# A windowed-attention kernel with its matmul groups in another order, the norm's short steps on GpSimd, and its last slots drawn by hand

## The chip, the cores and the metric

The kernel runs on one core of one Trainium2 chip. The metric is the device time of one execution in microseconds (us); lower is better. All data are 32-bit floats but for small masks.

## What is computed

First comes a layer of plain causal attention (16 heads of 64, model width 128) on x of shape 4 x 512 x 128, with a layernorm ahead of it. Then come six layers of local attention, each with a feed-forward part (FFN):

```python
for i in range(DEPTH):                      # 6
    x = attn_layer(shift_tokens(x), ...) + x
    x = ffn_layer(shift_tokens(x), ...) + x
# attn_layer: q, k, v = x @ Wqkv; q, k l2-normed per head, scaled, rotated;
#   windows of 32 queries see 64 keys; softmax; times v; @ Wo
# ffn_layer: layernorm; hg = xn @ W1 + b1; a * gelu(gate) @ W2 + b2   (341 wide)
```

`shift_tokens` moves half of the 128 channels by one token. The result of these layers is added to their input.

## The kernel before, in words

A **unit** is 128 tokens of one sequence in one layer of local attention: 6 layers x 4 sequences x 4 tiles (T = 0 to 3) = 96 units. Each unit takes three **slots**. In slot n, `slot` (L840) works on up to four units at once: `new` (n+2) is projected to q, k and v and rotated; `nxt` (n+1) has its q and k transposed; `u` (n) gets scores, exponents, product with V; `prev` (n-1) goes through wo and gets its residual. Everything runs under a manual schedule: each engine executes its instructions in the order of the program text, so the order of the calls in `slot` is the order of the work.

TensorE (PE) runs, per slot: `scores` (L643: 8 mask matmuls and 64 small ones, recorded as 128), `do_project` for q, `project_out_2` (L714, wo), `do_project` for v, `transpose_p` (L680), `do_project` for k, the first half of the product with V (`times_v`, L685: 32 small matmuls a half, recorded as 64), `transpose_q` (L627), the second half, `transpose_k` (L632), and `transpose_o` (L709). Between these stand parts of an FFN. An FFN belongs to a whole sequence (512 tokens, four units) and is spread over seven slots: shift in T=0, `mean` in T=1, `var` in T=2, `scale` in T=3, GEGLU chunks 0, 1, 2 at the ends of the slots T=3, 0, 1, and `out` at the end of the slot T=2. So each slot holds one GEGLU chunk or the output of some FFN, and all but T=0 one step of norm.

PSUM: three tiles of two banks (`two0` to `two2`), turned by one each slot by `part`, hold scores, q, k, v, both halves of the product with V, and the GEGLU chunks (`two_t`, L492; `project` uses (1, 2, 0) for q, k, v). One-bank tiles (`one_t`, L496, two in turn) hold wo's output, norm's results and four-block transposes: wo's output takes one, and the second half of `transpose_p` (L622, `transposed`) takes the same bank two allocations later.

VectorE (DVE) runs the maximum and the subtraction of the scores (L670, L672), sums of squares (L530), residuals (L725), rotations (L535, L539), the division after V (L701, L702), the starts of the inverse norms (L554, L80, L81), and the FFN's gates. ScalarE (ACT) runs squares (L525), exponents (L678), copies out of PSUM (L604, L625) and gelu. GpSimd (POOL) runs `add_rotated` (L550), the twelve steps L83 to L86 of `rsqrt` for the norms of q and k (`inverse_norms`, L552), `over_norm` (L558) and `carry_k` (L641). In the FFN's norm the same twelve steps are on DVE. SyncE (SP) issues the DMAs: 14 to 16 for each unit's V windows (L612 to L616), and the weights of the next layer after the last use of each.

The loop goes on for 7 slots after the last unit's, in which only the rest of the last FFNs is left; `finish` (L773) adds the layers' input, transposes and stores.

Of the kernel before, what the change touches and what calls it, by code (L numbers as in the profile page):

```python
# [32 lines left out]
def body(ctx: ExitStack, tc: tile.TileContext, a, out: bass.AP):  # L33
# [41 lines left out]
    def rsqrt(v, n, eng):  # L75

        y = small.tile([P, n], F32, tag=f"y{n}", name="y")
        t = small.tile([P, n], F32, tag=f"yt{n}", name="yt")
# [9 lines left out]
    def layernorm_steps(state, bank, inT, outT, g=None, b=None, eng=nc.vector):  # L88

        def mean():
            m = bank()
            mm(m, lhsT=avg, rhs=inT(), start=True, stop=True)  # L94
            xc = state["xc"] = tmpt()
            nc.vector.tensor_tensor(xc, inT(), m, ALU.subtract)
            sq = state["sq"] = tmpt()
            nc.scalar.activation(sq, xc, AF.Square)

        def var():  # L100
            v = bank()
            for t in range(NT):
                mm(v[:, t : t + 1], lhsT=state["sq"][:, t * P : (t + 1) * P], rhs=avg[:, 0:1], start=True, stop=True)  # L103
            rs = state["rs"] = small.tile([P, NT], F32, tag="rs", name="rs")
            nc.vector.tensor_scalar(rs, v[:, 0:NT], EPS, None, ALU.add)
            rsqrt(rs, NT, eng)

        def scale():
            bc = bank()
            for t in range(NT):  # L110
# [34 lines left out]
    def shift_into(dst, src):  # L145
# [3 lines left out]
        nc.gpsimd.tensor_copy(dst[HD:P, 1:S], src[HD:P, 0 : S - 1])  # L149
# [361 lines left out]
    def project(u, j):  # L511
        p = two_t((1, 2, 0)[j], "ps_proj")
# [172 lines left out]
    def times_v(u, g):  # L685
        if g == 0:
            u.on = s2.tile([P, NC, 2, HD], F32, tag="on", name="on", bufs=1)
        o = two_t(g, "ps_att")
# [41 lines left out]
    class Ffn:  # L730
        def __init__(self, i, b):
            self.i, self.b, self.us, self.st = i, b, [], {}
# [4 lines left out]
                lambda: s2.tile([P, S], F32, tag="hT", name="hT", bufs=2),  # L737
                vecs[:, i, 0:1],
                vecs[:, i, 1:2],
            )  # L740

        def shift(self):
            self.xs = tmpt()
            shift_into(self.xs, xT[self.b])

        def chunk(self, f):
            i, (f0, fn), h = self.i, FCH[f], self.st["h"]
            w1 = ffn_w[0][0]
            gp = two_t(0, "ps_proj")
            mm(gp[0:fn, 0, :], lhsT=w1[:, DH + f0 : DH + f0 + fn], rhs=h, start=True, stop=True)  # L750
            mm(gp[0:fn, 1, :], lhsT=w1[:, f0 : f0 + fn], rhs=h, start=True, stop=True)  # L751
            g = tmpt()
            nc.scalar.activation(g[0:fn, :], gp[0:fn, 0, :], AF.Gelu, bias=vecs[0:fn, i, 6 + f : 7 + f])
            u = tmpt()
            nc.vector.scalar_tensor_tensor(
                u[0:fn, :], gp[0:fn, 1, :], vecs[0:fn, i, 3 + f : 4 + f], g[0:fn, :], ALU.add, ALU.mult
            )
            self.us.append(u)

        def out(self):  # L760
            w2 = ffn_w[0][1]
            y = two_t(0, "ps_proj")[:, 0, :]
            for f, (f0, fn) in enumerate(FCH):
                mm(y, lhsT=w2[0:fn, f, :], rhs=self.us[f][0:fn, :], start=(f == 0), stop=(f == len(FCH) - 1))  # L764
            xn = new_xT()
            nc.vector.scalar_tensor_tensor(xn, y, vecs[:, self.i, 2:3], xT[self.b], ALU.add, ALU.add)
            xT[self.b] = xn
            if self.i + 1 == L:
                self.finish(xn)
            elif self.b + 1 == B:  # L770
                ffn_w[0] = load_ffn(self.i + 1)

        def finish(self, xn):  # L773
            fin = tmpt()
            nc.vector.tensor_tensor(fin, x1T[self.b], xn, ALU.add)
            op = one_t()
            for t in range(NT):
                nc.tensor.transpose(op[:, t * P : (t + 1) * P], fin[:, t * P : (t + 1) * P], ident)
            ot = tmpt()
            nc.scalar.copy(ot, op)  # L780
            nc.sync.dma_start(
                out=out[self.b].rearrange("(t p) e -> p t e", p=P),
# [57 lines left out]
    def slot(n, now, last):  # L840
# [4 lines left out]
        T = n % NT  # L845
        part[0] = n % 3
        begin(unit(n + 4))
        if u:
            scores(u)
        if new:  # L850
# [5 lines left out]
        if u:  # L856
            exponents(u)
# [4 lines left out]
        if new:  # L862
            sum_squares(new, 0)
        if prev:
            residual(prev)
        if now and T > 0:
            (now.mean, now.var, now.scale)[T - 1]()
        if now and T == 0:
            now.shift()
        if new:  # L870
            rotate(new, 0)
        if n == -1:
            residual1(B - 1, y)
        if new:
            do_project(new, 2)
            v_windows(new, follower(new))
        if u:
            transpose_p(u)
        if new:
            add_rotated(new, 0)  # L880
            do_project(new, 1)
            square(new, 1)
        if u:
            times_v(u, 0)
        if new:
            sum_squares(new, 1)
        if nxt:
            transpose_q(nxt)
        if u:
            times_v(u, 1)  # L890
        if new:
            inverse_norms(new)
            over_norm(new, 0)
        if nxt:
            transpose_k(nxt)
        if new:
            rotate(new, 1)
            add_rotated(new, 1)
            over_norm(new, 1)
# [4 lines left out]
        if now and T == 3:  # L904
            now.chunk(0)
        if last:
            (lambda: last.chunk(1), lambda: last.chunk(2), last.out)[T]()
# [3 lines left out]
    with tc.manual_schedule():  # L911
        begin(units[0])
        ffns = {}
        late = norm_x1(one_t, B - 1)
        first_slot()
        for n in range(-1, len(units) + NT + 3):
            if 1 <= n < 4:
                late[n - 1]()
            q = n // NT - 1
            if n % NT == 0 and 0 <= q < L * B:  # L920
# [95 lines left out]
```

## Time and profile before

| what | value |
|---|---|
| median of 3 runs | 2271.33 us (2264.25 to 2271.35) |
| profiled execution | 2271.15 us, its span 2269.1 us |
| granted TensorE clock | 0.992 |
| PE, DVE, POOL, ACT busy | 96%, 75%, 64%, 60% of the span |
| slot of unit 4 starts, slot of unit 88 starts | 639.45, 2099.09 us |
| slot of unit 94 starts | 2206.40 us |

The plain attention takes the first 570 us or so and is the same in both kernels. After it slots follow each other every 16 to 19 us. In the rows of a timeline, the first number is the start in us from the span's start, the second the length; "[0.80 <-DVE t L539]" is idle time of that engine just before the row, and what ended it. "issue" stands for idle time in which the engine waited for nothing that the profile shows. Ends of matmuls are modelled.

### The profile page before, as it was taken

How to read it: one execution, taken by the hardware profiler on the slowest of the kernel's cores; microseconds unless marked ns; L12 is line 12 of the kernel's file. 1: busy time of each engine (PE TensorE's matmuls, PEld its weight loads, DVE VectorE, ACT ScalarE, POOL GpSimd, SP SyncE). 2: the span in 40 equal slices, each digit the busy share in tenths (PEclk: the TensorE clock that was granted, in tenths of full speed). 3: DMA queues.
4: the chain of work that ended last, by engine and by line, in shares of the span. 5: the costliest groups of instructions: out<-in, count | busy, mean ns of one | idle time of the engine just before them, and what ended most of it. 6: DMA issues, size and time to landing. Idle time of an engine off the chain costs nothing.

```text
span 2269.1 us, 82300 instructions
## 1 busy us (share of the span) xinstructions
PE 2179.3 (96%) x35130; PEld 1443.3 (64%) x35130; DVE 1709.7 (75%) x2778; ACT 1361.3 (60%) x2582; POOL 1453.4 (64%) x1981
## 2 busy tenths in 40 slices
PE   7999999999899999999999999999999999999997
PEld 5565655554666666666666666666666666666664
DVE  3676667676777878878888788877888888878774
ACT  3665656564546656665656666566656666656662
POOL 2554545465777767677767776677776777766760
PEclk8999999999999999999999999999999999999999
DMA  3000000000322232232322233222332223223220
GB/s 116 1 1 1 1 1 1 1 1 9 85 58 65 69 87 67 65 74 65 94 62 65 70 80 86 62 69 60 87 79 61 71 65 92 69 62 73 66 59 15
DMA packets 91046, 125.76 MB, mean 55 GB/s; under 512 B 25406, under 2 KB 39484, under 8 KB 90684
## 3 DMA queue, kind: packets, MB, share of 16 engines
q1 hardware_dynamic: 89980, 118.79, 21.3%
q8 instruction: 280, 4.59, 0.9%
q10 hardware_dynamic: 704, 1.70, 0.2%
q14 instruction: 82, 0.67, 0.1%
HBM read 20.31 MB, written 1.05 MB: 9 GB/s over the span
## 4 chain that ended last, share of the span: by engine, by line
PE 64%; DVE 9%; issue 2%; ACT 1%; POOL 0%; ACTq 0%; POOLq 0%
PE ps_proj L514 19%; PE ps_one L622 13%; PE ps_one L717 7%; PE ps_att L692 6%; PE ps_att L660 6%; PE ps_proj L750 3%; PE ps_proj L751 3%; PE ps_proj L764 3%; DVE yt L80 2%; DVE t L539 1%; DVE rot L535 1%; PE ps_att L649 1%; PE ps_one L94 1%; PE ps_one L103 1%; DVE y L81 1%
## 5 line engine op out<-in xcount | busy, mean ns | idle before, releaser
L550 POOL TENSOR_TENSOR rot<-rot,t 128x1024 f32<-128x1024 f32 x192 | 454.1, 2365 | 204.4 <-DVE t L539 187.2
L514 PE MATMUL ps_proj<-wqkv,xs 128*128 128x512 f32 x1152 | 556.7, 606 | 6.3 <-DVE t L539 4.7
L525 ACT ACTIVATE sq<-ps_proj 128x1024 f32<-128x1024 f32 x192 | 196.9, 1025 | 363.9 <-PE ps_proj L514 315.3
L341 POOL TENSOR_TENSOR pr<-pr,den 128x1024 f32<-128x1024 f32 x128 | 241.1, 1894 | 250.0 <-DVE den L338 242.1
L558 POOL TENSOR_TENSOR rot<-rot,ss 128x1024 f32<-128x1024 f32 x192 | 365.4, 1903 | 14.9
L514 PEld LDWEIGHTS ps_proj<-wqkv,xs 128*128 128x128 f32 x1152 | 199.0, 191 | 169.4 <-issue 148.7
L530 DVE TENSOR_REDUCE ss<-sq 128x16 f32<-128x1024 f32 x192 | 233.1, 1214 | 49.5 <-ACT sq L525 48.8
L535 DVE TENSOR_TENSOR rot<-ps_proj,lt 128x1024 f32<-128x1024 f32 x192 | 233.6, 1217 | 0.0
L539 DVE TENSOR_TENSOR t<-ps_proj,lt 128x1024 f32<-128x1024 f32 x192 | 233.2, 1214 | 0.4 <-POOL rot L550 0.4
L327 ACT ACTIVATE pr<-ps_sc,nm 128x128 f32<-128x128 f32 (+3 forms) x448 | 220.6, 511 | 5.8 <-DVE nm L314 5.4
L314 DVE TENSOR_REDUCE nm<-ps_sc 128x2 f32<-128x1024 f32 x128 | 156.1, 1219 | 84.7 <-PE ps_sc L302 84.7
L717 PEld LDWEIGHTS ps_one<-aT,wo 128*128 128x128 f32 x1536 | 186.6, 192 | 45.8 <-issue 45.0
L622 PE MATMUL ps_one<-ident,rot 128*128 128x128 f32 x1536 | 209.9, 279 | 3.1 <-issue 2.2
L83 POOL TENSOR_TENSOR yt<-y 128x32 f32<-128x32 f32 (+1 forms) x309 | 73.3, 237 | 209.9 <-DVE y L81 170.0
L670 DVE TENSOR_REDUCE mx<-ps_att 128x16 f32<-128x1024 f32 x96 | 117.5, 1224 | 103.2 <-PE ps_att L660 102.4
L717 PE MATMUL ps_one<-aT,wo 128*128 128x128 f32 x1536 | 187.3, 275 | 0.4 <-ACT aT L625 0.4
L622 PEld LDWEIGHTS ps_one<-ident,rot 128*128 128x128 f32 x1536 | 164.6, 141 | 21.9 <-issue 4.4
L692 PEld LDWEIGHTS ps_att<-vw,pT 64*32 64x32 f32 x9216 | 103.5, 105 | 95.5 <-ACT pT L625 54.0
L604 ACT COPY vt<-ps_proj 128x512 f32<-128x512 f32 x192 | 103.2, 590 | 93.6 <-PE ps_proj L514 92.0
L692 PE MATMUL ps_att<-vw,pT 64*32 64x65 f32 x9216 | 129.4, 225 | 26.3 <-DVE t L539 13.8
L352 PEld LDWEIGHTS ps_pt<-ident,pr 128*128 128x128 f32 x1024 | 118.1, 142 | 57.0 <-issue 47.1
L701 DVE RECIPROCAL rden<-ps_att 128x8 f32<-128x8 f32 x192 | 38.9, 203 | 145.0 <-PE ps_att L692 144.9
(148 smaller groups left out, 4108.4 us busy)
## 6 DMA issues: line engine op xcount, KB each, us to landing
vw<-vt SPq DMA_DIRECT2D x1152, 65.0 KB
vw_first<-vt SPq DMA_DIRECT2D x336, 65.0 KB
wqkv<-in_wqkv_dram SPq DMA_DIRECT2D x18, 512.0 KB
wo<-in_wo_dram SPq DMA_DIRECT2D x6, 512.0 KB
w<-in_w_dram SPq DMA_DIRECT2D x6, 341.0 KB
out_dram<-tmp_t SPq DMA_DIRECT2D x4, 256.0 KB
xr<-in_x_dram SPq DMA_DIRECT2D x3, 256.0 KB
scales<-in_scales_dram SPq DMA_DIRECT2D x6, 128.0 KB
```

The lines of the kernel that those rows point to most:

```text
L327: nc.scalar.activation(self.pr[:, h, cols], self.sc[:, h, cols], AF.Exp, bias=self.nm[:, part_, h : h + 1], accum_out=self.den[:, part_, h ...
L341: nc.gpsimd.tensor_tensor(self.pr, self.pr, self.den[:, 0].unsqueeze(2).to_broadcast([P, 2, S]), ALU.mult)
L514: mm(p[:, c, :], lhsT=u.xs[:, u.T * P : (u.T + 1) * P], rhs=wpart[j][:, c * 512 : (c + 1) * 512], start=True, stop=True,)
L525: nc.scalar.activation(u.sq, u.p[j], AF.Square)
L530: nc.vector.tensor_reduce(u.ss[:, j * HEADS : (j + 1) * HEADS], heads(u.sq), AX.X, ALU.add)
L535: nc.vector.tensor_tensor(heads(t0), heads(pf), lt[:, u.T, 2 * j].unsqueeze(1).to_broadcast([P, HEADS, HD]), ALU.mult)
L539: nc.vector.tensor_tensor(t1.rearrange("p (h t d) -> p h t d", t=2, d=half), pf.rearrange("p (h t d) -> p h t d", t=2, d=half)[:, :, ::-1, :],
L550: nc.gpsimd.tensor_tensor(u.r[j], u.r[j], u.t1, ALU.add)
L558: nc.gpsimd.tensor_tensor(heads(u.r[j]), heads(u.r[j]), u.ss[:, j * HEADS : (j + 1) * HEADS].unsqueeze(2).to_broadcast([P, HEADS, HD]), AL ...
L622: nc.tensor.transpose(tp[:, c * P : (c + 1) * P], src[:, (4 * g + c) * P : (4 * g + c + 1) * P], ident)
L692: mm(o[j * W : (j + 1) * W, h, c * (HD + 1) : (c + 1) * (HD + 1)], lhsT=u.pT[h * HD : (h + 1) * HD, 4 * g + c, j * W : (j + 1) * W], rhs=u ...
L717: mm(y[:, 0:P], lhsT=wo_w[0][:, c, :], rhs=u.aT[:, c, :], start=(c == 0), stop=(c == NC - 1))
```

## The change

The calls in `slot` are put in another order, GEGLU chunks and the FFN's norm are planned in dictionaries by slot (`norm`, `move`, `geglu`), the twelve steps of the FFN norm go to GpSimd, and the slots from unit 95's on are written out as `tail`, in which the last sequence's FFN is split into its first three tiles (`most`) and its last (`last`).

```diff
     def project(u, j):
-        p = two_t((1, 2, 0)[j], "ps_proj")
+        p = two_t((1, 2, 1)[j], "ps_proj")
...
-    def times_v(u, g):
-        o = two_t(g, "ps_att")
+    def times_v(u, g, k=0):
+        o = two_t(k, "ps_att")
...
-            gp = two_t(0, "ps_proj")
+            gp = two_t(k, "ps_proj")
...
+                nc.scalar.copy(xs[0:HD, :], src[0:HD, c0 : c0 + n])
+                nc.scalar.copy(xs[HD:P, :], src[HD:P, c0 - 1 : c0 + n - 1])
...
+    def slot(n, norm, move, geglu):
         if u:
             scores(u)
+            exponents(u)
         if new:
             do_project(new, 0)
             square(new, 0)
-        if u:
-            exponents(u)
+        for f in norm:
+            f()
         if prev:
             project_out_2(prev)
...
-        if new:
-            sum_squares(new, 0)
-        if prev:
             residual(prev)
-        if now and T > 0:
-            (now.mean, now.var, now.scale)[T - 1]()
-        if now and T == 0:
-            now.shift()
+        for f in move:
+            f()
+        if u:
+            transpose_p(u)
         if new:
             rotate(new, 0)
-        if new:
-            do_project(new, 2)
-            v_windows(new, follower(new))
-        if u:
-            transpose_p(u)
-        if new:
             add_rotated(new, 0)
+            sum_squares(new, 0)
             do_project(new, 1)
             square(new, 1)
         if u:
             times_v(u, 0)
-        if new:
-            sum_squares(new, 1)
         if nxt:
             transpose_q(nxt)
+        if new:
+            do_project(new, 2)
+            v_windows(new, follower(new))
+            rotate(new, 1)
+            add_rotated(new, 1)
         if u:
             times_v(u, 1)
         if new:
-            inverse_norms(new)
-            over_norm(new, 0)
+            sum_squares(new, 1)
         if nxt:
             transpose_k(nxt)
-        if new:
-            rotate(new, 1)
-            add_rotated(new, 1)
-            over_norm(new, 1)
         if nxt:
             carry_k(nxt, follower(nxt))
-        if now and T == 3:
-            now.chunk(0)
-        if last:
-            (lambda: last.chunk(1), lambda: last.chunk(2), last.out)[T]()
+        if new:
+            inverse_norms(new)
+            over_norm(new, 0)
+            over_norm(new, 1)
+        for f in geglu:
+            f()
         if u:
             transpose_o(u)
...
+        for n in range(NT, end - NT, NT):
+            f = Ffn(units[n - 1], eng=nc.gpsimd)
+            plan(move, n, f.shift)
+            for k, g in enumerate((f.mean, f.var, f.scale)):
+                plan(norm, n + 1 + k, g)
+            for k in range(3):
+                plan(geglu, n + 3 + k, at(f.chunk, k, 2))
+            plan(geglu, n + 6, at(f.out, 2, n + 6 == end - 2))
...
+        plan(norm, end - 2, seq.var, *geglu.pop(end - 2))
+        plan(geglu, end - 2, early_scores, third.finish)
+        def tail():
+            exponents(u)
+            seq.scale()
+            project_out_2(prev)
+            residual(prev)
+            most.shift()
+            transpose_p(u)
+            most.mean()
+            part[0] = 1
+            times_v(u, 0, 0)
+            times_v(u, 1, 1)
+            part[0] = 0
+            gate = seq.chunk(0, 0, True)
+            transpose_o(u)
+            gate()
+            most.var()
+            project_out_2(u)
+            residual(u)
+            last.shift()
+            seq.chunk(1, 1)
+            last.mean()
+            most.scale()
+            last.var()
+            seq.chunk(2, 2)
+            for k in range(2):
+                most.chunk(k, k)
+            last.scale()
+            most.chunk(2, 2)
+            seq.out(0, True)
+            for k in range(3):
+                last.chunk(k, (k + 1) % 3)
+            seq.finish()
+            most.out(1, True)
+            last.out(2, True)
+            most.finish()
+            last.finish()
```

In the plan the GEGLU chunks and the output use k = 2. The two `nc.scalar.copy` lines are the shift of an FFN part that doesn't start at token 0. `third` and `seq` are the FFNs of the second and the third sequence of the last layer.

## The prediction, as it was put on record

> **What bounds it now.** I read the shares first: TensorE (PE) is busy 96% of the span, VectorE (DVE) 75%. So only a wait that holds PE is worth anything. Next, PE's own waits: PE column, then total us, times, longest.
>
> ```profile
> PE ps_att L692 <- DVE t L539: 13.8, 19, 0.9
> PE ps_att L692 <- issue: 13.1, 17, 1.4
> PE ps_att L660 <- issue: 8.9, 18, 1.7
> PE ps_proj L514 <- DVE t L539: 4.7, 8, 1.3
> ```
>
> The reader sees that 19 times the second half of the product with V (L692) stood until the rotation of q (L539) was off its bank; that the two groups of many small matmuls (L692, L660) stood for nothing that shows; and that the rest is small. Then the timeline of PE in one slot with T=2 (start, length):
>
> ```profile
> 2132.49 0.41 PE L649 MATMUL ps_att<-band,ident 64*32 64x512 bf16 x8
> 2132.72 1.69 PE L660 MATMUL ps_att<-kT,qT 64*32 64x64 f32 x128
> 2134.34 1.98 PE L514 MATMUL ps_proj<-wqkv,xs 128*128 128x512 f32 x4
> 2136.16 1.95 PE L717 MATMUL ps_one<-aT,wo 128*128 128x128 f32 x16
> 2137.94 0.95 PE L103 MATMUL ps_one<-avg,tmp_t 128*128 128x1 f32 x8
> 2138.76 1.96 PE L514 MATMUL ps_proj<-wqkv,xs 128*128 128x512 f32 x4
> 2140.55 1.04 PE L622 MATMUL ps_one<-ident,pr 128*128 128x128 f32 x8
> 2141.43 1.88 PE L514 MATMUL ps_proj<-wqkv,xs 128*128 128x512 f32 x4
> 2143.24 0.86 PE L692 MATMUL ps_att<-vw,pT 64*32 64x65 f32 x64
> 2144.03 1.09 PE L622 MATMUL ps_one<-ident,rot 128*128 128x128 f32 x8
> 2145.93 0.86 PE L692 MATMUL ps_att<-vw,pT 64*32 64x65 f32 x64 [0.80 <-DVE t L539]
> 2146.72 1.09 PE L622 MATMUL ps_one<-ident,rot 128*128 128x128 f32 x8
> 2147.65 2.74 PE L764 MATMUL ps_proj<-tmp_t,w 128*128 128x512 f32 x6
> ```
>
> Ends are modelled, so I price a group by start to next start: band and scores 1.85, q 1.82, wo 1.78, variance 0.82, P's transposes 0.88, k 1.81, each V half 0.79, k's transposes 0.93; from other slots v 1.72, q's transposes without the wait 1.02, a GEGLU chunk 1.71, output matmul 2.58, o's transposes 0.97, mean 0.86, scale 0.44. A slot with a chunk and no norm is 16.07; four slots are 4 x 16.07 + 0.86 + 0.82 + 0.44 + 0.87 = 67.3 us. Slot starts 639.45 and 2099.09, 21 periods apart, give 69.5. So 2.2 us a period, some 50 us of the whole, is all the waiting there is: 0.8 in T=2 (the row above), about 0.8 gaps in the V halves, 0.4 at the scores, 0.2 at P's transposes in T=0 (ScalarE, ACT, still in the exponent).
>
> The rows of DVE and GpSimd (POOL) in that slot say why L539 was late:
>
> ```profile
> 2139.13 1.75 DVE L80 TENSOR_SCALAR yt<-rs 128x4 int32<-128x4 int32 x1
> 2140.92 0.31 DVE L81 TENSOR_SCALAR y<-yt 128x4 int32<-128x4 int32 x1
> 2138.96 1.90 POOL L558 TENSOR_TENSOR rot<-rot,ss 128x1024 f32<-128x1024 f32 x1
> 2140.80 0.40 POOL L641 COPY kT<-kT 128x256 f32<-128x256 f32 x1
> ```
>
> L80 ends 0.02 after POOL's L558, L81 0.03 after L641; alone each takes 0.18. L117, 0.55 alone, has a median of 1.39. After these L83 to L86 hold DVE 12 x 0.2 = 2.4 us.
>
> The end: the last slots hold PE 47.5 of 64 us from 2206, with waits such as
>
> ```profile
> 2240.96 0.60 POOL L148 COPY tmp_t<-xT 64x512 f32<-64x512 f32 x1 [20.00 <-DVE xT L725]
> 2253.42 2.07 PE L750 MATMUL ps_proj<-hT,w 128*128 128x512 f32 x2 [1.36 <-DVE hT L117]
> ```
>
> The last sequence's whole FFN starts only after the last unit.
>
> **What the Trainium skill says.** "SBUF — State Buffer", Who interferes with whom: tensor_scalar in SBUF and GpSimd share a port pair that is locked for a whole instruction; the L80 rows agree. "Runtime: NRT & Kernel Launch", Instruction fetch mechanics: instructions are fetched in blocks of 256 ahead of use. The issue gaps agree in place (two records per small pass: 256 in the scores, 128 in each V half), but no row proves it. "PSUM — Partial Sum Buffer", PSUM bank collisions: two engines may not read one bank at once; so the new order makes rotate wait for square, now behind the exponent.
>
> **The change, part by part** (t is us from the band's start).
>
> *Bands of matmuls apart.* Same matmuls, another order: nominal stays 67.3. Between the V halves now lie q's transposes and v (2.8 us, not 1.0), so 256 instructions from the first half on take 4.2 us in place of 2.5. I take the V gaps (0.8) and, as most score gaps follow a V gap by 5.5 us, 0.3 of the scores' as gone. Bounds: nothing gained, or 1.2 and no more; below nothing, 0.3, if a gap moves to the scores.
>
> *Banks.* The second half reuses the first half's bank, free at about 11 by L702; it starts at 12 to 13: hidden, 1 us to spare. The 0.8 of T=2 and most of the q wait (L539, 0.2 a period) go, as rotate of k now precedes the norms of q and k; a chunk follows L539 by 0.5 to 1. The gate ends 0.95 into the next slot, q starts at 1.85.
>
> *Exponent ahead of square.* Exponent ends at 5.5 (maximum 1.95, subtraction to 4.42, 1.06); P's transposes are due at 5.4 in T=0, later elsewhere: 0.15, against 0.2 before. Square ends 6.5, so rotate of q starts there: v, due at 10, does not see it. Table loads (1.28) lie in ACT's idle time before.
>
> *v later.* Its two copies and 14 to 16 DMA issues (0.63 each) move from 7.5 to 12.4 and end at 6 of the next slot. Behind them on SP's queue stands the next layer's q weight, due 12.7 us later, 512 KB, some 5 us at the 100 GB/s or so of a full slice: hidden. V's windows have over a slot left.
>
> *Norm on GpSimd: the new wait.* The 12 steps leave DVE (2.4) for POOL, 12 x 0.32 = 3.9. POOL was idle 36%: hidden. But norm now stands ahead of the residual on DVE, and v no longer stands between wo and P's transposes, whose second half needs the residual's bank (two banks). What is queued behind L80, L81 and L117 is then the residual, and PE waits for it. POOL's order is new too: both over_norms run back to back after the 12 steps of inverse_norms, at the next slot's start. In T=1: second half's division ends 14.4, sum of squares 15.5, three port-bound steps held by add_rotated and carry to 16.4, POOL 3.9 + 3.8 to 24.1, which is 7.2 in T=2 (T=1 is 16.95). L80 at 4.8 meets the first over_norm, L81 the second: DVE free at 7.2, residual 7.5; second half of P due at 6.67: wait 0.86. In T=3 over_norm ends at 6.1, L117 0.3 later, residual 6.6 against 6.3: 0.34. T=1: 0.05. Bounds: 0 (no hold; not below, as 67.3 holds no wait) to 2.2 (each a further 0.5 late).
>
> Sum per period: 67.3 + 0.15 + 0.05 + 0.86 + 0.34 + 0.1 of gaps left = 68.8, against 69.5: 0.7 x 23 = 16 us.
>
> *End.* Its PE work from slot 94: scores twice 3.8, V halves 3.2, wo three times 5.4, transposes of p, q, k, o 5.6, chunks of three FFN parts 5.1 + 3.8 + 1.3, outputs 5.2 + 1.9 + 0.6, norms, mean to scale, 3.3, final transposes 1.4: 41 us in all. Waits: residual behind norm and the port 1.6, shift 1.0, two norms on POOL (3.9, not 2.4) 0.9 and 1.1, the last sum on DVE 0.7, small ones 1: 47 to the last transpose. Copy and store 0.6 + 3.1 as before: 51, against 62.7 from 2206.40: 12 us. Bounds: 5 (each wait twice) and 16. The finish of sequence 0 still stalls slot 90, as before.
>
> Sum: 2271.15 (span 2269.1 and 2.05 around it; the median is 2271.33, so no correction) - 16 - 12 = 2243.
>
> **Rivals.**
> - *No hold at the residual* (POOL's norms finish sooner, or the residual slips in): 1.2 x 23 = 28 more, 2215. For: L81 is sometimes 0.18. Against: POOL ops run end to end.
> - *The gaps stay*: 0.8 x 23 = 18 back, 2261. For: the scores follow the same groups as before.
> - *Slower*: the hold grows. DVE has under 1 us to spare per slot; if its sum of squares ends 1 us later, over_norms end 1 us later, and T=2 and T=3 each lose 1 us more, 46 slots, 2289. It is slower than 2271 from 0.6 us on. For: it feeds back, as the wait delays the next inverse_norms. Against: the hold ends with POOL's two ops, and T=0 has room to recover.
> - *It doesn't do what it says*: excluded; the built order on PE shows the groups apart.
>
> **How the numbers follow.** Forecast 0.45, no hold 0.20, gaps stay 0.20, slower 0.15. The measurement tells 0.3%, 7 us, from nothing. Faster by more (under 2264.5): 0.45 + 0.20 + half of the gaps case = 0.75; slower (over 2278) 0.13; same 0.12. Low end 2213: the no-hold case. High end 2272: the gaps case with 7 for the end's bound and half of what gaps may cost below nothing (0.3 x 23 / 2 = 3.5); it leaves out the slower case and a little below 2213.
>
> **What would show it.** Right: no wait of L692 on L539; few issue gaps at the V halves; a wait of P's transposes on the residual in T=2 (0.9) and T=3 (0.3); period 68.8; slot 94 to the end 51. Wrong: a period over 69.5, P waiting over 1 us in T=0 or T=1, chunk or q waiting for DVE, or issue gaps as before.

## The result, and the profile after

| | kernel before | changed kernel |
|---|---|---|
| median of 10 runs each | 2269.64 us (2264.25 to 2275.43) | 2259.68 us (2250.18 to 2264.64) |
| ratio after to before | | 0.9952, 95% interval 0.9938 to 0.9966 |
| profiled execution's span | 2269.1 | 2259.6 |
| start to the slot of unit 4 | 639.45 | 634.94 |
| unit 4 to unit 88 (21 periods of four slots) | 1459.64 | 1462.11 |
| unit 88 to unit 94 | 107.31 | 106.02 |
| unit 94 to the end | 62.70 | 56.53 |

It is faster by 10 us, where 28 were forecast. In this section and the next a period is four slots, from a slot with T=0 to the next such slot. Sixteen of the 21 periods are ordinary. In the other five the sequence is the last of the four, and the tables of the next layer are made in them (`layer_tables`, called by `begin`); I call these boundaries. From the slot starts of the trace, an ordinary period takes 69.01 us (before 69.50; the mean of the fifteen from unit 8 on), a boundary 71.87 (before 69.90). Of the 4.5 us in the row of unit 4, 2.5 lie ahead of the first projection of the local layers (542.19 us before, 539.69 after), in work that is the same in both kernels. They are not the change's.

Line numbers of the changed kernel are 3 to 23 higher: L625 transposes, L663 scores, L695 product with V, L517 projections, L728 residual, L542 the second half of a rotation, L771 gate. The waits of PE after, in the same columns as before:

```profile
PE ps_one L625 <- DVE xT L728: 17.5, 44, 1.4
PE ps_att L663 <- issue: 5.7, 10, 1.3
PE ps_proj L517 <- DVE tmp_t L771: 5.0, 4, 2.5
...
PE ps_att L695 <- issue: 0.9, 1, 0.9
```

The wait of V's second half on the rotation (13.8) is gone, the waits on "issue" fell from 25.3 to 7.4 in all, and a new wait stands on top: P's transposes wait for the residual 44 times. Here it is in a slot with T=2 (start, length, engine):

```profile
1996.95 2.03 PE L720 MATMUL ps_one<-aT,wo 128*128 128x128 f32 x16
...
1999.89 0.65 PE L625 MATMUL ps_one<-ident,pr 128*128 128x128 f32 x4 [0.47 <-DVE xT L728]
...
1997.32 0.46 DVE L81 TENSOR_SCALAR yt<-rs 128x4 int32<-128x4 int32 x1
1997.82 1.82 DVE L82 TENSOR_SCALAR y<-yt 128x4 int32<-128x4 int32 x1
1999.56 0.28 DVE L728 TENSOR_TENSOR xT<-ps_one,xT 128x128 f32<-128x128 f32 x1
...
1995.85 3.76 POOL L561 TENSOR_TENSOR rot<-rot,ss 128x1024 f32<-128x1024 f32 x2
```

The two products of `over_norm` run on POOL from 1995.85 to 1999.61. L82 ends 0.03 after them, 7.0 us into the slot (7.2 forecast), and the residual, queued behind L82, starts only then. That was forecast. What was not forecast is a boundary. Rows of POOL, DVE and PE in the slot with T=0 that starts at 1328.92, and in the next one, at 1345.22:

```profile
1332.19 3.76 POOL L561 TENSOR_TENSOR rot<-rot,ss 128x1024 f32<-128x1024 f32 x2
...
1339.45 2.37 POOL L164 TENSOR_TENSOR lt<-tabs,scales 128x1024 f32<-128x1024 f32 x1 [2.04 <-DMA scales<-in_scales_dram]
...
1343.35 4.68 POOL L553 TENSOR_TENSOR rot<-rot,t 128x1024 f32<-128x1024 f32 x2
...
1345.79 2.28 DVE L81 TENSOR_SCALAR yt<-ss 128x32 int32<-128x32 int32 x1
...
1348.32 0.74 DVE L771 SCALAR_TENSOR_TENSOR tmp_t<-ps_proj,vecs,tmp_t 128x512 f32<-128x512 f32 x1
...
1349.11 3.68 PE L517 MATMUL ps_proj<-wqkv,xs 128*128 128x512 f32 x4 [1.75 <-DVE tmp_t L771]
```

POOL does `over_norm` twice, a shift, waits for `scales`, makes the table, does the FFN's shift, and reaches the sums of the rotated halves (L553) only 14.4 us into the slot. L81 waits behind these sums, the gate behind L81, and q's projection for the gate. So the next slot takes 20.84 us in place of some 17.1 (18.2 to 21.5 at the five boundaries).

### The profile page after: what moved, and what is told of

Read it like the earlier page. It is cut to its first block, busy times and chain, and to the rows that moved or that the text cites. A ratio compares the mean times of both kernels' runs of the same rounds, so it can differ in the third digit from the quotient of the medians.

```text
span 2259.6 us, 82472 instructions
## 1 busy us (share of the span) xinstructions
PE 2183.4 (97%) x35150; PEld 1435.4 (64%) x35150; DVE 1710.3 (76%) x2501; ACT 1365.9 (60%) x2589; POOL 1511.7 (67%) x2281
## 3 DMA queue, kind: packets, MB, share of 16 engines
q1 hardware_dynamic: 89996, 118.79, 21.4%
## 4 chain that ended last, share of the span: by engine, by line
PE 58%; DVE 12%; POOL 3%; issue 2%; ACT 1%; POOLq 0%; ACTq 0%
PE ps_proj L517 18%; PE ps_one L625 14%; PE ps_att L663 6%; PE ps_att L695 6%; PE ps_one L720 3%; PE ps_proj L783 3%; PE ps_proj L763 3%; PE ps_proj L764 3%; DVE y L82 2%; DVE mx L673 2%; DVE pr L675 2%; PE ps_att L652 1%; DVE hT L120 1%; POOL rot L553 1%; DVE t L542 1%
## 5 line engine op out<-in xcount | busy, mean ns | idle before, releaser
L553 POOL TENSOR_TENSOR rot<-rot,t 128x1024 f32<-128x1024 f32 x192 | 453.9, 2365 | 255.8 <-DVE t L542 188.5
L517 PE MATMUL ps_proj<-wqkv,xs 128*128 128x512 f32 x1152 | 557.0, 606 | 5.9 <-DVE tmp_t L771 5.0
L517 PEld LDWEIGHTS ps_proj<-wqkv,xs 128*128 128x128 f32 x1152 | 197.5, 191 | 157.2 <-issue 143.2
L681 ACT ACTIVATE pr<-pr 128x1024 f32<-128x1024 f32 x96 | 101.5, 1058 | 260.8 <-DVE pr L675 260.8
L542 DVE TENSOR_TENSOR t<-ps_proj,lt 128x1024 f32<-128x1024 f32 x192 | 233.2, 1215 | 19.6 <-POOL rot L553 19.2
L538 DVE TENSOR_TENSOR rot<-ps_proj,lt 128x1024 f32<-128x1024 f32 x192 | 233.0, 1214 | 19.5 <-ACT sq L528 19.4
L625 PE MATMUL ps_one<-ident,rot 128*128 128x128 f32 x1536 | 209.6, 279 | 0.9 <-POOL rot L561 0.9
L625 PEld LDWEIGHTS ps_one<-ident,rot 128*128 128x128 f32 x1536 | 164.7, 141 | 19.8 <-POOL rot L561 1.1
L695 PEld LDWEIGHTS ps_att<-vw,pT 64*32 64x32 f32 x9216 | 101.1, 105 | 108.3 <-issue 108.0
L84 POOL TENSOR_TENSOR yt<-y 128x32 f32<-128x32 f32 (+2 forms) x384 | 88.0, 229 | 93.6 <-DVE y L82 47.5
L355 PE MATMUL ps_pt<-ident,pr 128*128 128x128 f32 x1024 | 135.7, 275 | 3.0 <-POOL pr L344 2.7
```

The costliest lines, as they stand in the source:

```text
L355: nc.tensor.transpose(pt[:, k * P : (k + 1) * P], self.pr[:, h, k * P : (k + 1) * P], ident)
L517: mm(p[:, c, :], lhsT=u.xs[:, u.T * P : (u.T + 1) * P], rhs=wpart[j][:, c * 512 : (c + 1) * 512], start=True, stop=True,)
L538: nc.vector.tensor_tensor(heads(t0), heads(pf), lt[:, u.T, 2 * j].unsqueeze(1).to_broadcast([P, HEADS, HD]), ALU.mult)
L542: nc.vector.tensor_tensor(t1.rearrange("p (h t d) -> p h t d", t=2, d=half), pf.rearrange("p (h t d) -> p h t d", t=2, d=half)[:, :, ::-1, :],
L553: nc.gpsimd.tensor_tensor(u.r[j], u.r[j], u.t1, ALU.add)
L625: nc.tensor.transpose(tp[:, c * P : (c + 1) * P], src[:, (4 * g + c) * P : (4 * g + c + 1) * P], ident)
```

## The experiments

Each ran beside the kernel before on the same chip; ratios are to that kernel, with 95% intervals. The segments come from each run's own trace:

| run | ratio | ordinary period | boundary | unit 94 to end |
|---|---|---|---|---|
| before | 1 | 69.50 | 69.90 | 62.70 |
| changed kernel | 0.9952 (0.9938 to 0.9966) | 69.01 | 71.87 | 56.53 |
| load of scales early | 1.0003 (0.9995 to 1.0011) | 68.96 | 72.92 | 56.79 |
| load and table early | 0.9916 (0.9899 to 0.9932) | 69.01 | 68.88 | 55.87 |
| four t1 tiles | 0.9931 (0.9910 to 0.9953) | 68.74 | 70.48 | 57.07 |
| residual first | 0.9952 (0.9935 to 0.9970) | 69.03 | 70.63 | 56.41 |
| residual first, table early | 0.9918 (0.9904 to 0.9931) | 68.90 | 68.83 | 56.44 |
| residual first, begin early, four t1 | 0.9830 (0.9817 to 0.9843) | 68.18 | 67.93 | 55.46 |
| v back | 1.0287 (1.0271 to 1.0303) | 71.51 | 74.94 | 56.69 |
| halves close, table early | 1.0003 (0.9993 to 1.0012) | 69.52 | 69.36 | 56.64 |
| before, norm on GpSimd | 0.9918 (0.9902 to 0.9934) | 68.80 | 69.02 | 63.94 |
| before, norm on GpSimd, new end | 0.9919 (0.9902 to 0.9936) | 68.71 | 68.95 | 58.85 |
| new order, norm on VectorE | 1.0255 (1.0232 to 1.0278) | 72.26 | 75.25 | 55.35 |
| table early, end's norm on VectorE | 0.9927 (0.9914 to 0.9940) | 68.96 | 68.87 | 55.39 |
| all three edits, early gelu | 0.9805 (0.9792 to 0.9819) | 68.18 | 68.04 | 54.02 |
| all three edits, output apart | 0.9815 (0.9799 to 0.9831) | 68.18 | 68.26 | 59.41 |
| all three edits, both | 0.9805 (0.9791 to 0.9819) | 68.08 | 68.06 | 54.60 |

"All three edits" are residual first, begin early and four t1 tiles.

### What holds the boundaries

My first theory was the wait on the DMA in the rows above: v's window transfers now stand ahead of the `scales` load on SP's queue. The load alone was moved, into the `begin` four slots before:

```diff
-            lt = layer_tables(u.i) if u.b == 0 else units[u.n - 1].lt
+            lt = layer_tables(u.i, early_scales[0]) if u.b == 0 else units[u.n - 1].lt
+        if u.b + 1 == B and u.i + 1 < L:
+            early_scales[0] = load_scales(u.i + 1)
```

> The changed kernel, but with the load of the next layer's `scales` issued four slots earlier, ahead of the transfers for V's windows that it stood behind; the table's product on GpSimd stays where it was. Theory A (moving v behind the transposes of q put V's window transfers ahead of the `scales` load on SP's queue, and GpSimd waits 2 us for it at each of five layer boundaries): the wait of `lt` on the DMA goes, the five boundary periods fall from about 72 us to 69.5 to 70.5, and the time is 8 to 14 us under the changed kernel's 2259.7, about 2249. Theory B (it is the table's own 2.4 us on GpSimd, in new company there, or the weights' loads, that hold the boundary): under 4 us gained, about 2257, and the boundary periods stay above 71.

Theory A fell. The wait on the DMA is gone, the boundary is longer, 72.92, and the whole is as slow as the kernel before (1.0003); only the late slot is another (T=0, 18.9 to 21.5 us). That the boundary is longer, and not just as long, is TensorE's clock (last section). A boundary of this run:

```profile
1343.79 2.38 POOL L168 TENSOR_TENSOR lt<-tabs,scales 128x1024 f32<-128x1024 f32 x1
...
1347.71 2.35 POOL L557 TENSOR_TENSOR rot<-rot,t 128x1024 f32<-128x1024 f32 x1
...
1350.09 1.23 DVE L546 TENSOR_TENSOR t<-ps_proj,lt 128x1024 f32<-128x1024 f32 x1 [2.92 <-POOL rot L557]
...
1351.37 2.07 PE L767 MATMUL ps_proj<-hT,w 128*128 128x512 f32 x2 [2.38 <-DVE t L546]
```

The table still stands ahead of the sum of q's halves, which ends at 1350.06. The rotation of k waits for that sum, by the three t1 tiles (squares, second halves) that they share, as I read it here (a run below bears it out); the chunk (L767) waits for k's bank. So the transfer only covered the next thing in line, GpSimd itself. Next the table's product moved too, to the slot with T=3 ahead, behind `move`:

```diff
+        ahead = unit(n + 5)
+        if ahead and n > 0 and ahead.b == 0 and ahead.T == 0:
+            early_tables[0] = layer_tables(ahead.i, early_scales[0])
         if u:
             transpose_p(u)
```

> The changed kernel with the `scales` load four slots earlier, as in the run that moved only the load, and also the table's product on GpSimd (2.4 us) moved from the start of the boundary's slot with T=0 into the slot with T=3 ahead of it, where GpSimd is idle for some 6 to 9 us. Theory A (at a boundary GpSimd has both over_norms, a shift, the table and the FFN's shift ahead of the sum of q's halves, and everything behind that sum is late): the five boundary periods fall from about 72 to 69.5 us, the time is 11 to 15 us under the changed kernel, a ratio to the kernel before of 0.989 to 0.991. Theory B (the excess is due to something else at the boundary, such as the weights' loads): under 4 us gained, a ratio of 0.994 or more.

Theory A holds: the five boundaries take 68.88 us, no more than other periods, and units 4 to 88 take 15.2 us less than in the changed kernel's trace. By the ratios (0.9916 against 0.9952) the gain is 8 us, with some 5 of uncertainty, where 11 to 15 were expected: the traces are one execution each. The table in its new place:

```profile
1311.94 2.56 POOL L168 TENSOR_TENSOR lt<-tabs,scales 128x1024 f32<-128x1024 f32 x1
...
1332.62 2.36 POOL L557 TENSOR_TENSOR rot<-rot,t 128x1024 f32<-128x1024 f32 x1
```

The sum of q's halves of the boundary's T=0 (slot start 1322.77) now starts 9.9 us into the slot. The link by t1 was tried by itself, with `bufs=4` for 3 at both tiles t1:

> The changed kernel with four buffers in place of three for the tiles t1 (squares, and the second halves of the rotations), so that the rotation of k need not wait for GpSimd's sum of q's halves to free one. Theory A (VectorE is tied to GpSimd's lateness through these three buffers): at the boundaries the rotation of k no longer waits for GpSimd, and some 5 to 12 us go, a ratio to the kernel before of 0.990 to 0.993. Theory B (the lateness reaches TensorE by q's and k's finished tiles in any case): within 3 us of the changed kernel, a ratio of 0.994 to 0.9965.

Boundaries fell from 71.87 to 70.48 and the ordinary periods by 0.27; units 4 to 88 take 13 us less. The ratio is at the edge of A's range, and its interval reaches the changed kernel's: the time alone does not show the gain, and the profiled execution was the fastest of six. What shows the link is a wait of VectorE that the changed kernel has and this run has not at all:

```profile
DVE t L542 <- POOL rot L553: 19.2, 41, 3.0
```

So the link by t1 is real, but GpSimd's lateness also comes through other ways: two of the five boundaries still had a slot of 19.5 and 21.4.

### The residual's hold, and what stands behind it

```diff
-            rsqrt(rs, nt, eng)
+            now_or_held(lambda: rsqrt(rs, nt, eng))
...
-                nc.vector.tensor_scalar(h, h, g, b, ALU.mult, ALU.add)
+                now_or_held(lambda: nc.vector.tensor_scalar(h, h, g, b, ALU.mult, ALU.add))
...
             residual(prev)
+        for f in held:
+            f()
```

Here `now_or_held` puts the start of the norm's inverse root, with GpSimd's steps behind it, and the scaling by g and b off until the residual is out.

> The changed kernel, but VectorE does the residual ahead of the norm's three instructions that wait for GpSimd's port (the two that start the inverse root, and the scaling by g and b); PE's order is untouched. Theory A (the residual is held on VectorE behind these three, and P's transposes wait for it): the wait of P's transposes on the residual, 17.5 us in the profile, falls under 4, the slots with T=2 and T=3 lose 0.5 each, and the time is 18 to 24 us under the changed kernel's 2259.7, about 2239. Theory B (VectorE and GpSimd are late as such, so the same wait comes out at the next thing that needs VectorE, the rotation of q or the chunk): under 8 us gained, about 2254, and waits on the rotation (L538, L542) or the gate grow by what the residual's wait lost.

The hold is as the prediction has it: with the residual ahead, it is gone from PE's list of waits, T=2 falls from 18.39 to 17.99 and T=3 from 17.01 to 16.69 (medians). But T=0 rises from 16.34 to 17.10, the chunk's wait for the rotation of k grows from 1.6 to 8.3 us, and the time is that of the changed kernel: theory B.

```profile
PE ps_proj L771 <- DVE t L550: 8.3, 16, 0.8
```

With the table early as well:

> The two earlier edits together: the residual ahead of the norm's port-bound instructions on VectorE, and the layer's table one slot earlier on GpSimd. Theory A (two separate costs, the table at five boundaries, some 15 us, and the residual's hold, of which 0.7 a period goes and 0.75 comes back in T=0, where GpSimd's two shifts stand ahead of the sum of q's halves): T=2 near 18.0, T=3 near 16.7, T=0 still near 17.1, and a ratio to the kernel before of 0.990 to 0.992, as with the table alone. Theory B (the wait in T=0 was the boundary's lateness carried on): T=0 returns to 16.3, and the ratio is 0.983 to 0.985.

Theory A again: T=0 stays at 17.16, the chunk waits for the rotation of k 21 times (12.2 us), and the gain is the table's alone. A slot with T=0, start 1940.55:

```profile
1951.19 2.36 POOL L565 TENSOR_TENSOR rot<-rot,t 128x1024 f32<-128x1024 f32 x1
...
1953.59 1.23 DVE L554 TENSOR_TENSOR t<-ps_proj,lt 128x1024 f32<-128x1024 f32 x1 [1.01 <-POOL rot L565]
...
1954.87 1.13 PE L775 MATMUL ps_proj<-hT,w 128*128 128x512 f32 x2 [0.49 <-DVE t L554]
```

Ahead of the sum L565 POOL has two `over_norm` (to 1948.3) and two shifts (to 1951.1), one of `begin` and one of the FFN. So in ordinary periods, too, GpSimd in T=0 was next in line behind the residual. The `begin` (shift and table) was therefore moved to T=3, and t1 got four tiles:

```diff
-        begin(unit(n + 4))
+        if n == 0:
+            begin(unit(4))
...
         for f in move:
             f()
+        if n > 0:
+            begin(unit(n + 5))
```

> As the run with both edits, but the shift that begins a sequence is moved from T=0 to the T=3 slot ahead too (with the table), and the tiles t1 have four buffers, so that in T=0 the sum of q's halves has one shift ahead of it and not two, and the rotation of k need not wait for it. Theory A (T=0's new wait comes from GpSimd's shifts): T=0 falls to 16.2 to 16.5 with T=2 and T=3 kept at 18.0 and 16.7, the period is 68.0 to 68.3, the ratio to the kernel before 0.982 to 0.986. Theory B (something else, such as the gelu's path, is due in T=0): T=0 stays above 16.9 and the ratio is 0.989 or more.

T=0 is back at 16.33 with T=2 at 18.05 and T=3 at 16.67: theory A. Summed over its list of waits PE waits 38.3 us in the whole execution, against 71.4 in the changed kernel. How much of this the shift and the fourth t1 tile each bring was not separated; VectorE's wait for GpSimd's sum of q's halves, 37.2 us in the run before this one, is gone from its list.

### The gaps without a cause

Here v's projection and transfers went back between the residual and P's transposes, and the second half of the product with V took bank k=1:

> The changed kernel, but v's projection and its window transfers stand again between the residual and P's transposes, so that only the transposes of q lie between the two halves of the product with V; V's second half takes the bank of q. Theory A (the idle times of PE without a cause in the profile come with many small matmuls too close together): idle time of that kind rises from 6 us to 18 to 24 us and stands again at V's halves and the scores; the wait of P's transposes on the residual (17.5) goes, as v fills it, and the layer boundaries recover some 10 as the window transfers are early again: about 2247 to 2253 in all. Theory B (those idle times had to do with something else in the old order): they stay near 6 us, and the time is about 2232.

```profile
PE ps_proj L763 <- DVE t L542: 45.5, 52, 3.6
PE ps_att L695 <- issue: 14.8, 16, 1.5
...
PE ps_att L663 <- issue: 9.9, 18, 1.5
```

The idle time without a cause rose to 26.9 us, 14.8 of it at V's halves and 9.9 at the scores (13.1 and 8.9 in the kernel before), and the wait on the residual fell to 2.0: theory A for both. The time is far from either theory, since v had also stood between k's projection and the chunk: without it the chunk waits 45.5 us for the rotation of k. The boundaries were no shorter with v's transfers early (3.4 over the ordinary period). To part these, v's projection alone changed sides with V's second half, in the kernel with the early table; the two take the banks of the old order with it (v k=0, the second half k=1):

```diff
-            do_project(new, 2)
-            v_windows(new, follower(new))
             rotate(new, 1)
             add_rotated(new, 1)
         if u:
-            times_v(u, 1)
+            times_v(u, 1, 1)
         if new:
+            do_project(new, 2)
+            v_windows(new, follower(new))
```

> The changed kernel with the table one slot earlier, and only v's projection moved by one group: behind the second half of the product with V, not ahead of it, so that the halves have only the transposes of q between them, while all else keeps its place. Theory A (idle time of TensorE without a cause comes with two halves and scores too close together): such idle time rises from 6 to 18 to 24 us and stands at the V halves again; the ratio to the kernel before is 0.996 to 1.000, against 0.9916 with the table alone. Theory B (these gaps belonged to something else of the old order): 4 to 8 us of such idle time, a ratio of 0.991 to 0.993.

```profile
PE ps_att L667 <- issue: 15.8, 23, 1.5
...
PE ps_att L699 <- issue: 1.0, 2, 0.7
```

The idle time rose from 7.2 to 18.4 us and the ratio by 0.009, so A's amount holds; but it stands at the scores (L667), not at V's halves (L699). So the order brings these gaps or takes them away. That the small groups' distance does it fits all runs, but isn't shown alone: every run that has the gaps also has v and the second half in these banks of the old order, though no wait for a bank shows at them. That instructions are fetched too late then, as the prediction took it, fits too and is not shown.

### The parts by themselves

The kernel before, with `nc.gpsimd` as the engine of the FFN's norm and nothing else:

> The kernel before, with only the twelve steps of the inverse root in the FFN's norm moved from VectorE to GpSimd. Theory A (the wait of V's second half on the rotation of q, 13.8 us, came from 2.4 us of these steps on VectorE): that wait falls under 4, the wait of q's projection on the rotation of k (4.7) shrinks too, and the time is 10 to 16 us under the kernel before, about 2257. Theory B (the steps take 3.9 us on GpSimd, where the sum of the rotated halves and the inverse norms queue behind them, and the three port-bound instructions still hold VectorE): under 5 us gained, or a loss, about 2268.

```profile
PE ps_att L692 <- issue: 14.1, 18, 1.5
...
PE ps_proj L514 <- DVE t L539: 4.7, 7, 1.1
```

Theory A in the main, and more than its 10 to 16 us: the wait of V's second half on the rotation is gone, and 19 us with it. The wait of q's projection, which was to shrink, stayed at 4.7. This one edit beats the changed kernel (0.9918 against 0.9952). With the hand-drawn end added to the old order:

> The order of the slots as before the change, with v ahead of P's transposes and the norm behind the residual, but with the norm's steps on GpSimd (as in the run of the kernel before with that alone) and the end drawn by hand as in the changed kernel. Theory A (the three parts add up: the norm on GpSimd is worth some 19 us in the old order, the end 6, and the new order of the slots loses what it gains): 5 to 8 us under the run with the norm alone, a ratio to the kernel before of 0.988 to 0.990. Theory B (the hand-drawn end lives on the new order): no better than the norm alone, a ratio of 0.992 or more.

Inconclusive: the trace has an end of 58.85 against 63.94, but the ratio is the same, and the two intervals are each 0.003 wide. And the new order with the norm on VectorE in the loop:

> The changed kernel with the twelve steps of the FFN norm's inverse root back on VectorE in all slots but those drawn by hand. Theory A (the residual now stands behind the norm on VectorE, so the new order needs the norm off VectorE): in T=2 the wait of P's transposes on the residual grows from 1.4 to some 3.5 us, and the time is 25 to 50 us over the changed kernel, a ratio to the kernel before of 1.006 to 1.018. Theory B (the hold by GpSimd's port sets the residual, and the steps fit in beside it, with GpSimd freer by 3.9 us a period): within 8 us of the changed kernel, a ratio of 0.992 to 0.999.

```profile
1919.46 0.28 DVE L728 TENSOR_TENSOR xT<-ps_one,xT 128x128 f32<-128x128 f32 x1
...
1919.80 0.66 PE L625 MATMUL ps_one<-ident,pr 128*128 128x128 f32 x4 [2.62 <-DVE xT L728]
```

Theory A: the twelve steps now lie between L82 and the residual, T=2 rises to 22.24 (median), and the boundaries keep their 3 us of excess. The ratio is above A's range, and the waits are only part of it: in units 4 to 88 the trace has 16 stretches of 3.41 us at half clock, which is some 27 us of the 66 by which they are longer than in the changed kernel (last section). The new order lives on the norm being on GpSimd; the norm on GpSimd doesn't need the new order. Whether the old order would gain from an earlier begin and a fourth t1 tile as the new one does was not run, so what the new order itself is worth stays open.

### The end

The changed kernel's end, PE and ACT:

```profile
2216.11 0.54 PE L695 MATMUL ps_att<-vw,pT 64*32 64x65 f32 x34 [0.91 <-issue]
...
2220.22 0.74 PE L663 MATMUL ps_att<-kT,qT 64*32 64x64 f32 x51 [1.26 <-issue]
...
2231.53 1.28 ACT L767 ACT_TABLE_LOAD   x1 [2.37 <-PE ps_proj L764]
...
2234.04 0.83 PE L106 MATMUL ps_one<-avg,rot 128*128 128x1 f32 x6 [1.72 <-ACT aT L628]
```

First the two norms of the last sequence went back to VectorE (`most` and `last` with `nc.vector`, on top of the early table):

> The changed kernel with the table one slot earlier, and in the end drawn by hand the inverse roots of the last sequence's two norms on VectorE, not on GpSimd. Theory A (in the end nothing covers the steps, which take 3.9 us on GpSimd and 2.4 on VectorE): the end from slot 94 on shrinks by 1 to 3 us against the run with the table alone (ratio 0.9916 there), 0.990 to 0.991 here. Theory B (the end is set by TensorE's own work, its small gaps and ScalarE's table loads): the end stays within 0.7 us.

Theory B: 55.39 against 55.87. Then, on the version with all three edits, a gelu of one column behind the copies of P:

```diff
             transpose_p(u)
+            early_gelu = small.tile([P, 1], F32, tag="early_gelu", name="early_gelu")
+            nc.scalar.activation(early_gelu, vecs[:, 0, 0:1], AF.Gelu)
             most.mean()
```

> The run with the residual first, the sequence's begin one slot earlier and four t1 tiles, and in its end one gelu of a single column on ScalarE behind the copies of P, whose result nobody reads, so that gelu's table is loaded before the first chunk's matmuls are done. Theory A (the table's load of 1.3 us waits for these matmuls, and the copies of o, with the variance behind them, wait for it): the wait of the variance on the copies of o (1.7 us) falls under 0.6, and slot 94 to the end takes 53.8 to 54.6 us, not 55.5. Theory B (the variance or what follows waits for another engine next): the wait moves, and the end stays within 0.5 of 55.5.

```profile
2191.26 1.28 ACT L1009 ACT_TABLE_LOAD   x1
...
2196.71 0.83 PE L114 MATMUL ps_one<-avg,rot 128*128 128x1 f32 x6 [0.44 <-ACT aT L640]
```

Theory A, to the size: 54.02 against 55.46, and the wait of the variance on the copies of o is down from 1.72 to 0.44. The load had waited for the chunk's matmuls together with its gelu, and the copies of o behind it. The Trainium skill, "ScalarE: Activation LUTs", What ACT_TABLE_LOAD costs, gives 1283 ns for the load; both traces have 1.28. The drain of some 1380 ns that it adds for each switch doesn't show here: the copies of P end at 2191.24, the load follows at 2191.26, and the early gelu starts at 2192.55. The ratio is 0.9805 (0.9792 to 0.9819) against 0.9830, the lowest here together with the last run's; the 1.4 us are about a quarter of that difference, and the rest isn't accounted for. The other edit took the early output matmuls out of `norm` in slot 94, so that they run behind k's transposes:

> The same run with residual first, begin earlier and four t1 tiles, and in its slot 94 the output matmuls of the third-to-last FFN stand between the transposes of k and the scores, not ahead of the product with the output weights. Theory A (the gap of 1.3 at these scores comes from groups of small matmuls too close together, as between V's halves): the gap at the scores goes or falls under 0.4, and the end takes 54.0 to 54.8, not 55.5. Theory B (the gap only moves, or the transposes of P now wait for the residual, which has less work ahead of it): the end stays within 0.5 of 55.5 or gets longer.

The gap at the scores went, but the end grew to 59.41: P's transposes now come before the exponent is done (0.79), the scores wait 0.84 for VectorE, a gap of 0.86 stands at V's second half. Another 3 us or so are half clock from 2199.62 to 2206.44, which this edit need not have caused (last section). Theory B in either case. Both edits:

> Both edits of the end together. Theory A (separate costs): 52.5 to 53.6 from slot 94 to the end, the ratio to the kernel before 0.981 to 0.9825, against 0.983 with neither. Theory B (one end behind the other: the chain of the last sequence's norm sets the end anyway): 54.5 or more.

54.60 us and 0.9805 (0.9791 to 0.9819): nothing over the gelu alone. The 2.2 us of gaps in the end are not won by this move; another was not tried.

## Why the prediction was right or wrong

The forecast was 28 us (16 in the steady state, 12 in the end), the trace has 9.5. The 18.5 that are missing are, but for rounding: 13.4 at the boundaries, where 5 x 0.7 were forecast and 9.9 were lost (5 x (71.87 - 69.90)); 5.8 in the end (12 - 6.2); 3.8 in the other 16 periods (11.2 - 7.4); less 4.4, as ahead of unit 4 and from unit 88 to 94 5.8 were won where 1.4 were forecast, some of it not the change's.

- **Right, with its size: the ordinary period.** 69.01 (68.9 from the medians of the four slots) for 68.8. V's wait on the rotation is gone, and the rotation of q now waits for the square, as it has it (19.4 us of VectorE's time; none before). The gaps fell by 18 us in the list of waits (25 were forecast, by starts: 1.1 x 23). Of the 18 at the scores only eight followed a gap at V by 5.4 to 5.9 us, so "most" was misread. And the residual's wait came: by starts P's transposes take 1.46, 1.35 and 1.04 us in T=2, T=3 and T=1 for a nominal 0.88, which is 1.21 a period. That this is so near the 1.25 forecast is partly luck: with the residual first the three still take 1.04, so 0.73 is the hold by the norm's instructions, and 0.16 in each is a short wait, for which the prediction has only the 0.05 in T=1. So the gaps' gain went into the residual's wait, and what is left came from the rotation's.
- **Right: the mechanism of the hold.** The runs with the residual first take it away (0.73 a period). But the rival "no hold", which gives 28 us more, is wrong in its price: without the hold GpSimd in T=0 is next in line, and nothing is gained until the shift is moved too.
- **Wrong, and the largest term: "POOL was idle 36%: hidden", and 0.7 us applied to all 23 periods.** This is the step that failed: GpSimd's queue at the start of T=0 was put at nothing. The prediction saw that both `over_norm` now run at the next slot's start, and carried this to L80 and L117 in T=1 to T=3 only. In T=0 the two shifts of `begin` and the FFN queue behind them, and at five boundaries the table of 2.4 us, all ahead of the sum on which VectorE and the t1 tiles depend. The early table, with its load, takes the whole excess away (15.2 us by the traces). A mean idle share said nothing of that slot. The rival "slower" even had it that T=0 has room to recover; when the residual came first, it was T=0 that grew, from 16.34 to 17.10.
- **Incomplete, but not the cause: "v later".** It named only q's weight behind v's transfers on SP's queue, and not the load of `scales`, which GpSimd waited for (14.9 us in all). With that load early nothing was won.
- **Wrong in size: the end.** The terms that were too small are PE's own groups. To the last transpose 53.1 us, where 47 were forecast; 3.4 after it (3.7 forecast). The waits sum to 8.0 in place of 6.3: gaps of 2.2 and the wait behind the table load, 1.7, were not in the list, while others were smaller. PE's own groups, by starts, take 45.1, not 41: transposes of p, q, k and o 6.8 for 5.6, the norms 4.4 for 3.3, chunks 10.9 for 10.2, V's halves 3.7 for 3.2, and so on, as prices from the packed loop don't hold between waits. Taking the norms' GpSimd steps as 2 us of waits was wrong; moving them was worth 0.5.
- **The rivals.** "The gaps stay" is out, 7.4 us being left. "Slower, as the hold grows" didn't come in T=2 and T=3; lateness of GpSimd did cost time, but by its queue in T=0, and at the boundaries in the slot after it.

## What to carry to other kernels

When work on a second engine is moved, write that engine's queue down for every kind of slot, the rare ones too, and find the first thing on it that others wait for; its mean idle share hides a slot in which it is full. When a wait is removed, ask which resource is due next and by how much: here the transfer, the residual and the rotation each covered GpSimd, and the gain came only when its own load was spread. Before a large change of order is judged, run its cheapest part alone: the norm on GpSimd in the old order gave 19 us, the whole change 10.

## What the runs showed that was not expected

TensorE can run at half speed after a wait shorter than 2 us. After the wait of 1.75 at 1349.11 four matmuls of q's projection took 3.68 us, not 1.98, and the granted clock fell. In the rows: a stretch, its length, busy time of PE with its instructions, then clock, DMA share, GB/s:

```profile
1345.82:1349.23 3.41, 1.41 (x109) 1.00 0.42 98
...
1349.23:1352.64 3.41, 3.41 (x5) 0.50 0.32 71
...
2229.87:2233.28 3.41, 2.45 (x12) 1.00 0.01 2
2233.28:2236.69 3.41, 2.40 (x20) 1.00 0.00 0
```

The Trainium skill, "TensorE: Matmul & The Clock Gate", Part 1: The HAM clock gate, states half rate after an idle window of about 3.4 us. Here PE was busy 1.41 of the 3.41 us before, with no single wait over 1.75, so less than a whole idle window was enough. Within the loop and the end, until PE has finished, half clock comes in stretches of 3.41 us or twice that, and each costs some 1.7 us where PE is busy throughout.

After a wait of 1.72 in the changed kernel's end, from 2232.32 to 2234.04, it did not happen. Of the 13 traces that have this same wait, of the variance on the copies of o, six have half clock right behind it. One is the run with the output apart; its output weights and those of the changed kernel, behind the same wait:

```profile
2200.25 3.78 PE L732 MATMUL ps_one<-aT,wo 128*128 128x128 f32 x16 [0.25 <-DVE rs L116]
2235.12 2.05 PE L720 MATMUL ps_one<-aT,wo 128*128 128x128 f32 x16 [0.25 <-DVE rs L108]
```

Where the wait falls may decide. Half clock stood from 2151.36 to 2154.77 in the changed kernel. In steps of 3.41 us counted from there a border falls on 2233.28, inside the wait, and PE is busy 2.45 and 2.40 us in the two stretches that share it; in the other run the stretch ahead of the half clock was busy 1.69. But this is no rule yet: in the run with the load early one was busy 1.51 (from 1070.97), and full clock followed.

So a wait can cost about twice its length. Two such stretches at the boundaries of the changed kernel are 3.4 of the 9.9 us that were lost there; with the load early there are five, 8.5 us, and the difference, 5.1, is about what those boundaries are longer. The early gelu takes away a wait that cost 1.7 us more in some executions and nothing more in others.
